# Expert weights on GpSimd's queue, and routing pieces that begin earlier in a group and lie further apart

## The chip, the core and the metric

The kernel runs on one core of one Trainium2 chip. A core has a matrix engine (TensorE, PE in the profile; its weight loads are PEld), VectorE (DVE), ScalarE (ACT), GpSimd (POOL) and SyncE (SP), which here only starts transfers. Each engine works through its own instructions in order and waits for the others by semaphores. Transfers between HBM and the on-chip memory, and within it, are started from the queue of SP, ACT or POOL and carried out by 16 DMA engines that all queues share. The metric is the device time of one execution in microseconds.

## The reference

The input x is 8 sequences of 256 tokens of width 256, in float32. Two blocks follow each other, and every sublayer adds to x:

```python
x = x + L0_xattn(layernorm(x), ctx)     # 16 heads of 16
x = x + L0_ffn(layernorm(x))            # soft mixture of 8 experts, 128 slots each
x = x + L1_xattn(layernorm(x), ctx)     # 16 heads of 64
x = x + L1_ffn(layernorm(x))            # gated square of relu
```

The change touches the second line only:

```python
xn = rmsnorm(x); sn = rmsnorm(slot_embeds)
logits   = einsum('bnd,esd->bnes', xn, sn)
dispatch = softmax(logits, over tokens n)
combine  = softmax(logits, over all e*s = 1024 slots)
slots = einsum('bnd,bnes->besd', xn, dispatch)
h     = gelu(einsum('besd,edh->besh', slots, w1) + b1)   # 256 -> 1024
eo    = einsum('besh,ehd->besd', h, w2) + b2             # 1024 -> 256
out   = einsum('bmd,bnm->bnd', eo, combine)
```

An expert has w1 and w2 of 1 MB each and b2 of 1 KB.

## The kernel before

The four sublayers run one after the other; x stays on the chip (`x_sb`). The instructions are written in a program order, and a planner then sets the order on each engine's queue: among what it holds for ready at a time, by its own estimate, the earlier in the program goes first. Only what is marked `keep_in_program_order` keeps its place. So an instruction that depends on nothing can stand much earlier in its queue than in the program, and a queue's order can differ from the code's.

**Groups.** The mixture handles the 8 sequences in 4 groups of two. All 8 experts run in each group, so each expert's weights are loaded four times. `experts(g)` gives 64 pieces, numbered n = 0 to 63, eight for an expert e. A piece is `up(e, hc)`, two products for 128 of the 1024 hidden units (L986) with a gelu on ScalarE into `ht` (L994), and one of the eight steps `down(e-1, k)` of the expert before (L1002), which waits in the list `late`. After the last step VectorE adds b2 and writes the result over `slots` (L1011).

**Weights.** There are two sets of weight buffers (`moe_sets`), used by even and odd experts, each with w1, w2 and b2. `load_second(e)` (w2 and b2: L221, L222) is written in piece 8e, `load_first(e + 1)` (w1: L218) in piece 8e + 1. All three are started from SP's queue. A load waits until TensorE has finished with the expert two before it, since that one used the same buffers. The first expert's weights are asked for at step 50 of the first sublayer's schedule, by `at(50, ...)`; they go to buffers that nothing used before.

**Routing.** `routing(g + 1)` prepares the next group's sequences (b = 0, 1 of the group) beside the experts of group g. Its steps are:

- P: normalised tokens, turned on TensorE (pt_xm).
- T: logits with tokens in rows (L851, `ln`), their maximum, an exponential on ScalarE (L862) with the reciprocal of its sum in `rzn`, and 32 x 32 transposes on VectorE (L810). The second T of a sequence also starts a *spread*: 16 transfers of 64 KB from `tk_l` to `ls` on SP's queue (L818), which bring the 32 x 32 blocks to their places.
- A: the same for the exponentials, with a spread of 16 transfers from `tk_n` to the matrix `CT` that combines the experts' outputs.
- S: softmax over tokens on half of the slots: maximum on VectorE (L893), four exponentials on ScalarE (L898), and a multiplication on GpSimd (L906).
- C: transposes back (L916) and a spread from `tk_s` to `dt`.
- F: the experts' inputs, `slots`, on TensorE (L931, `pf`) and VectorE (L941).

A sequence has two T and one A, two S and one C, and two F. A "-" in the list of steps is an empty place. `ending` holds the combining of the group before: four times eight products (L1028, `pc`) and the statistics of the next layernorm.

**Where side pieces go.** `side` is the list of ending and routing steps. One is taken after each odd n above 8; what is left over follows the last piece. With five steps of ending ahead of them in groups 1 to 3, the routing steps of groups 1 and 2 begin at n = 19; in group 0 they begin at n = 9.

Buffers that matter: `ls` and `dt` have one each; `tk`, the exponentials `em` and `rzn` two; `ph`, `pf` and `pt_xm` share three banks of the matrix engine's output memory with `pc`.

Of the kernel before, what the change touches and what calls it, by code (L numbers as in the profile page):

```python
# [14 lines left out]
P = 128  # L15
# [47 lines left out]
def kernel(ctx: ExitStack, tc: tile.TileContext, a: dict, out: bass.AP):  # L63
    nc = tc.nc
# [74 lines left out]
    def moe_mean(g):  # L139

        mv = stat.tile([P, 4, 2], F32, tag="mvp", bufs=4, name=f"mvp_moe_{g}")
        for i in range(4):
            st = stat.tile([P, 6], F32, tag="bst", bufs=4, name=f"bst_moe_{g}_{i}")
            nc.vector.bn_stats(st, x_sb[:, 4 * g + i, :])
            nc.vector.bn_aggr(mv[:, i, :], st)
        moe_stats[g] = mv

    def moe_scale(groups):


        got = []
        for g in groups:
            mv = moe_stats[g]
            roots = stat.tile([P, 2, 4], F32, tag="roots", bufs=3, name=f"roots_{g}")
            for i, (bias, scale) in enumerate(((epsb, 1.0), (0.0, float(D)))):
                tc.keep_in_program_order(
                    nc.scalar.activation(
                        roots[:, i, :], mv[:, :, 1], AF.Sqrt, bias=bias, scale=scale
                    )
                )  # L160
            got.append((g, mv, roots))
        for g, mv, roots in got:
            scl = stat.tile([P, 4], F32, tag="scl", bufs=3, name=f"scl_{g}")
            rstd = stat.tile([P, 4], F32, tag="rstdm", bufs=3, name=f"rstdm_{g}")
            nc.vector.reciprocal(rstd, roots[:, 0, :])
            nc.vector.tensor_tensor(scl, roots[:, 1, :], rstd, ALU.mult)
            nc.vector.tensor_scalar(scl, scl, 1e-12, None, ALU.max)
            nc.vector.reciprocal(scl, scl)
            nc.vector.scalar_tensor_tensor(scl, scl, 16.0, rstd, ALU.mult, ALU.mult)
            moe_stats[g] = mv, scl  # L170
# [44 lines left out]
        )  # L215

    def load_first(to, e):
        nc.sync.dma_start(to["w1"], a["w1"][e].rearrange("(c p) f -> p c f", p=P))  # L218

    def load_second(to, e):  # L220
        nc.sync.dma_start(to["w2"], a["w2"][e].rearrange("(c p) f -> p c f", p=P))  # L221
        nc.sync.dma_start(to["b2"], a["b2"][e].partition_broadcast(P))  # L222

    moe_sets = [moe_tiles(pr, 0)]
    with ExitStack() as l0:
# [534 lines left out]
        for b, plan in enumerate(  # L760
# [7 lines left out]
            does = dict(zip("PTUSDF", routing0(b)))  # L768
            for step in plan.split():
                when, _, args = step[1:].partition(".")  # L770
                at(int(when), lambda f=does[step[0]], args=args: f(*map(int, args)))
        at(50, lambda: load_first(set0, 0))
        at(50, lambda: load_second(set0, 0))

        turn_back, halves = None, []
# [23 lines left out]
    with ExitStack() as l0f:  # L799
# [22 lines left out]
        def routing(g):  # L822


            CT = moe_sets[g % 2]["CT"]
            rzn = stat.tile([P, 4], F32, tag="rzn", bufs=2, name=f"rzn_{g}")
# [3 lines left out]
            does = []  # L830
            for bl in range(2):
# [118 lines left out]
                    dict(P=prepare, T=by_token, A=turn_token, S=by_slot, C=turn_slot, F=fill)  # L950
                )

            pieces = []
            for step in (
                "P0 T00 T01 A0 P1 - S00 S01 C0 T10 T11 - F00 F01 A1 - S10 S11 C1 - - F10 F11"
            ).split():
                if step == "-":
                    pieces.append(lambda: None)
                else:
                    f, args = does[int(step[1])][step[0]], tuple(map(int, step[2:]))  # L960
                    pieces.append(lambda f=f, args=args: f(*args))
            return pieces, CT, rzn

        late = []

        def experts(g):
# [5 lines left out]
            def up(e, hc):  # L972
                w, n = moe_sets[e % 2], g * E + e

                if hc == 0 and n > 0:
                    load_second(w, e)
                if hc == 1 and n < 4 * E - 1:
                    load_first(moe_sets[(e + 1) % 2], (e + 1) % E)
                if hc == 0:
                    cur[e] = dict(w1=w["w1"], w2=w["w2"], b2=w["b2"], ht=[])  # L980
                c_ = cur[e]
                if hc % 2 == 0:
                    c_["ph"] = ps_mm(f"ph_{g}_{e}_{hc}").rearrange("p (i n) -> p i n", i=2)
                ph = c_["ph"][:, hc % 2, :]
                for c in range(2):
                    nc.tensor.matmul(  # L986
                        ph,
                        lhsT=c_["w1"][:, c, hc * P : (hc + 1) * P],
                        rhs=slots[e][:, c * 256 : (c + 1) * 256],
                        start=(c == 0),  # L990
                        stop=(c == 1),
                    )
                ht = pm.tile([P, 256], F32, tag="ht", bufs=14, name=f"ht_{g}_{e}_{hc}")
                nc.scalar.activation(ht, ph, AF.Gelu, bias=b1[:, e, hc : hc + 1])  # L994
                c_["ht"].append(ht)
# [49 lines left out]
        def finish(g, eos, CT, rzn):  # L1045
            pieces = [
                lambda bl=bl, t=t: combine(g, bl, t, eos, CT, rzn)
                for bl in range(2)
                for t in range(2)
            ]  # L1050

            def stats():
                xat_stats[g] = ln_pair(g, f"xat_{g}")

            return pieces + [stats]

        CT, rzn = set0["CT"], rzn0
        ending = []
        for g in range(4):
            work_, eos = experts(g)  # L1060
            here = (eos, CT, rzn)
            side = list(ending)
            if g < 3:
                if g == 2:
                    moe_mean(3)
                    moe_scale([3])
                pieces, CT, rzn = routing(g + 1)
                side += pieces
            for n, piece in enumerate(work_):
                piece()  # L1070
                if n % 2 == 1 and n > 8 and side:
                    side.pop(0)()
            for piece in side:
                piece()
            ending = finish(g, *here)
# [8 lines left out]
    with ExitStack() as l1:  # L1084
# [222 lines left out]
        to, qs, vs = projs[0]  # L1307
# [184 lines left out]
```

## Time and profile before

| | us |
|---|---|
| median of 3 runs | 1375.34 (1373.31 to 1376.81) |
| the profiled execution | 1375.42 |
| its span, first to last instruction | 1373.6 |
| TensorE busy | 1302.9 (95%) |
| VectorE busy | 572.2 (42%) |
| ScalarE busy | 564.2 (41%) |
| GpSimd busy | 194.8 (14%) |
| first expert product to last combining product | 283 to 912 |

The profile is one execution. In its lists of instructions each line gives the start in us from the span's beginning, the duration, engine, line of the kernel, operation, output<-input and count; brackets hold the idle time before it and what ended that. An engine name with q is that engine's queue: instructions that only start a transfer or wait. A line of waits reads: who waited, for whom, us in total, how often, the longest. In the strips of digits each digit is the busy share of a fortieth of the span in tenths.

### The profile page before, as it was taken

What the parts mean: (1) busy time and instruction counts of PE and PEld (TensorE: products, weight loads), DVE (VectorE), ACT (ScalarE), POOL (GpSimd) and SP (SyncE); (2) the same over time, 40 slices, a digit from 0 to 9 for tenths busy, and PEclk for the clock granted to TensorE, in tenths of its full rate; (3) what the DMA queues carried; (4) which work ended last, traced back from release to release, by engine and by line L of the source; (5) the groups of instructions that cost most, each with busy time, mean ns of one, the idle gap of its engine ahead of it and who ended that gap; (6) DMA issues with size and microseconds to landing.
All of it is one profiled execution on the core that took longest, in us unless ns stands there. A gap on an engine that the chain in (4) does not pass through costs nothing.

```text
span 1373.6 us, 18749 instructions
## 1 busy us (share of the span) xinstructions
PE 1302.9 (95%) x7216; PEld 937.8 (68%) x7216; DVE 572.2 (42%) x1160; ACT 564.2 (41%) x1374; POOL 194.8 (14%) x149
## 2 busy tenths in 40 slices
PE   6999999899989999799998999999999999999988
PEld 3566665466667877578767788866667667577767
DVE  5777777533311234221350210025444544554544
ACT  1445454636322245322553122204544544544643
POOL 1000001101010001100011000013332422323514
PEclk8899999999999999999998999999999999999999
DMA  8000000025664435752467524240000000000001
GB/s 259 14 2 1 1 2 1 1 96 142 183 171 144 131 98 146 190 190 82 119 166 186 169 93 168 100 126 0 1 1 1 1 1 1 1 1 1 1 31 54
DMA packets 125161, 105.72 MB, mean 77 GB/s; under 512 B 57105, under 2 KB 115089, under 8 KB 125073
## 3 DMA queue, kind: packets, MB, share of 16 engines
q1 hardware_dynamic: 123488, 103.22, 25.4%
q10 hardware_dynamic: 1584, 1.31, 0.4%
q8 instruction: 57, 0.93, 0.3%
q14 instruction: 32, 0.25, 0.1%
HBM read 83.53 MB, written 2.10 MB: 62 GB/s over the span
## 4 chain that ended last, share of the span: by engine, by line
PE 70%; SPq 9%; DMA 7%; ACT 6%; DVE 5%; issue 2%; POOL 1%; POOLq 0%; ACTq 0%; DVEq 0%
PE ph L986 11%; PE pe L1002 11%; SPq L818 8%; PE sc L73 8%; PE q L73 6%; PE o L73 5%; PE po L73 5%; PE k L73 5%; PE pc L1028 4%; DMA w<-in_w_dram 4%; PE v L73 4%; PE pe L76 4%; PE pf L931 2%; ACT ex L1228 2%; PE ln L851 1%
## 5 line engine op out<-in xcount | busy, mean ns | idle before, releaser
L994 ACT ACTIVATE ht<-ph,b 128x256 f32<-128x256 f32 x256 | 118.3, 474 | 386.7 <-PE ph L986 385.6
L1002 PE MATMUL pe<-w,ht 128*128 128x256 f32 x1024 | 262.5, 389 | 13.9 <-DMA w<-in_w_dram 13.9
L986 PE MATMUL ph<-slots,w 128*128 128x256 f32 x1024 | 264.6, 386 | 11.3 <-ACT ht L994 5.4
L986 PEld LDWEIGHTS ph<-slots,w 128*128 128x128 f32 x1024 | 187.7, 191 | 67.5 <-ACT ht L994 26.2
L1002 PEld LDWEIGHTS pe<-w,ht 128*128 128x128 f32 x1024 | 197.2, 194 | 48.4 <-issue 10.1
L1241 POOL TENSOR_TENSOR ex<-ex,rz 128x1024 f32<-128x1024 f32 x64 | 120.2, 1899 | 224.1 <-DVE rz L1239 219.5
L1228 ACT ACTIVATE ex<-sc,nm 128x256 f32<-128x256 f32 x256 | 117.4, 484 | 45.2 <-DVE nm L1223 44.0
L1011 DVE TENSOR_TENSOR slots<-pe,b 128x512 f32<-128x512 f32 x32 | 22.1, 691 | 269.1 <-PE pe L1002 269.1
L73 PE MATMUL sc<-KT,QT 17*128 17x256 f32 (+1 forms) x1024 | 106.3, 385 | 5.5 <-DVE NM L488 3.6
L499 ACT ACTIVATE ex<-sc 128x512 f32<-128x512 f32 x128 | 74.7, 597 | 83.8 <-PE sc L73 76.0
L488 DVE TENSOR_REDUCE NM<-sc 128x2 f32<-128x512 f32 x128 | 86.7, 687 | 31.8 <-PE sc L73 27.4
L73 PEld LDWEIGHTS sc<-KT,QT 17*128 17x128 f32 (+1 forms) x1024 | 78.0, 189 | 28.3 <-issue 13.3
L73 PE MATMUL q<-xT,wq 128*128 128x256 f32 x384 | 94.8, 395 | 0.9 <-ACT V L1193 0.9
L73 PEld LDWEIGHTS q<-xT,wq 128*128 128x128 f32 x384 | 70.9, 192 | 26.4 <-issue 12.1
L906 POOL TENSOR_TENSOR ls<-ls,zs 128x1024 f32<-128x1024 f32 x12 | 22.7, 1894 | 430.2 <-DMA CT<-tk_n 364.2
L1223 DVE TENSOR_REDUCE nm<-sc 128x4 f32<-128x1024 f32 x64 | 75.4, 1219 | 6.5 <-PE sc L73 2.8
L73 PE MATMUL po<-wo,ot 128*128 128x256 f32 x320 | 72.6, 382 | 0.0
L76 PE MATMUL pe<-ident,ex 128*128 128x128 f32 x512 | 69.9, 278 | 0.5 <-DVE xT L1143 0.4
L73 PEld LDWEIGHTS po<-wo,ot 128*128 128x128 f32 x320 | 60.1, 190 | 11.3 <-issue 3.6
L1257 ACT COPY et<-pe 128x512 f32<-128x512 f32 x64 | 37.1, 608 | 72.0 <-PE pe L76 71.7
L76 PEld LDWEIGHTS pe<-ident,ex 128*128 128x128 f32 x512 | 56.2, 140 | 14.1 <-issue 8.0
L73 PE MATMUL o<-et,V 128*64 128x256 f32 x512 | 62.8, 385 | 0.9 <-ACT ot L1276 0.9
(180 smaller groups left out, 1551.3 us busy)
## 6 DMA issues: line engine op xcount, KB each, us to landing
w<-in_w_dram SPq DMA_DIRECT2D x64, 1024.0 KB, 7.1
ls<-tk_l SPq DMA_DIRECT2D x96, 64.0 KB, 2.0
CT<-tk_n SPq DMA_DIRECT2D x96, 64.0 KB, 2.1
dt<-tk_s SPq DMA_DIRECT2D x96, 64.0 KB, 2.9
b<-in_b_dram SPq DMA_DIRECT2D x32, 128.0 KB, 6.9
out_dram<-y SPq DMA_DIRECT2D x8, 256.0 KB, 2.1
x_sb<-in_x_dram SPq DMA_DIRECT2D x3, 512.0 KB, 6.9
ctx0T<-in_ctxT_dram SPq DMA_DIRECT2D x4, 256.0 KB, 6.0
```

Source lines behind the costliest of these rows:

```text
L73: tc.keep_in_program_order(nc.tensor.matmul(out, lhsT=lhsT, rhs=rhs, start=start, stop=stop))
L76: tc.keep_in_program_order(nc.tensor.transpose(out, in_, ident))
L488: nc.vector.tensor_reduce(NMs[(2 * b + t // 2) % 2][:, qb, t, HD0 + 1 + 64 * i : 64 * i + 64 : 32], sc[i][:, :, 0, :], AX.X, ALU.max, nega ...
L499: nc.scalar.activation(ex[:, 2 - 2 * i : 4 - 2 * i, :], sc[1 - i][:, :, 1, :], AF.Exp)
L818: nc.sync.dma_start(to(32 * k, a), tk[32 * a : 32 * a + 32, k, :, :, :].rearrange(rows))
L986: nc.tensor.matmul(ph, lhsT=c_["w1"][:, c, hc * P : (hc + 1) * P], rhs=slots[e][:, c * 256 : (c + 1) * 256], start=(c == 0), stop=(c == 1),)
L994: nc.scalar.activation(ht, ph, AF.Gelu, bias=b1[:, e, hc : hc + 1])
L1002: nc.tensor.matmul(c_["pe"][:, b, :], lhsT=c_["ht"][hc][:, b * SL : (b + 1) * SL], rhs=c_["w2"][:, hc, :], start=(hc == 0), stop=(hc == HI ...
L1028: nc.tensor.matmul(pc[:, :D], lhsT=CT[:, bl, e, t * P : (t + 1) * P], rhs=eos[e][:, bl, :], start=(e == 0), stop=(e == E - 1),)
L1223: nc.vector.tensor_reduce(nm, sc, AX.X, ALU.max, negate=True)
L1228: nc.scalar.activation(ex[:, i, qb, :], sc[:, i, qb, :], AF.Exp, bias=nm[:, i, qb : qb + 1], accum_out=z[:, i, qb : qb + 1],)
L1241: nc.gpsimd.tensor_tensor(ex, ex, rz.rearrange("p h q -> p (h q)").unsqueeze(2).to_broadcast([P, 4, S]), ALU.mult,)
```

## The change

`load_first` and `load_second` start their three transfers from GpSimd's queue instead of SP's, for all experts and groups.

The list of routing steps is split. P0, T00 and T01 (the first sequence's tokens and logits) form `first`, which goes ahead of the ending of the group before; the rest follows the ending. In groups 0 to 2 side pieces are taken after each odd n above 2 instead of above 8, so that `first` stands after n = 3, 5 and 7 and three more places exist. They are used for further empty places in the list: one after S01, one between T10 and T11, one between S10 and S11 and one more after C1, while the one between T11 and F00 goes. In group 3, which has no routing, pieces are still taken from n = 9.

```diff
     def load_first(to, e):
-        nc.sync.dma_start(to["w1"], a["w1"][e].rearrange("(c p) f -> p c f", p=P))
+        nc.gpsimd.dma_start(to["w1"], a["w1"][e].rearrange("(c p) f -> p c f", p=P))
 
     def load_second(to, e):
-        nc.sync.dma_start(to["w2"], a["w2"][e].rearrange("(c p) f -> p c f", p=P))
-        nc.sync.dma_start(to["b2"], a["b2"][e].partition_broadcast(P))
+        nc.gpsimd.dma_start(to["w2"], a["w2"][e].rearrange("(c p) f -> p c f", p=P))
+        nc.gpsimd.dma_start(to["b2"], a["b2"][e].partition_broadcast(P))
...
+            def piece(step):
+                if step == "-":
+                    return lambda: None
+                f, args = does[int(step[1])][step[0]], tuple(map(int, step[2:]))
+                return lambda: f(*args)
+
+            first = [piece(step) for step in ("P0", "T00", "T01")]
             pieces = []
             for step in (
-                "P0 T00 T01 A0 P1 - S00 S01 C0 T10 T11 - F00 F01 A1 - S10 S11 C1 - - F10 F11"
+                "A0 P1 - S00 S01 - C0 T10 - T11 F00 F01 A1 - S10 - S11 C1 - - - F10 F11"
             ).split():
-                if step == "-":
-                    pieces.append(lambda: None)
-                else:
-                    f, args = does[int(step[1])][step[0]], tuple(map(int, step[2:]))
-                    pieces.append(lambda f=f, args=args: f(*args))
-            return pieces, CT, rzn
+                pieces.append(piece(step))
+            return first, pieces, CT, rzn
...
-                pieces, CT, rzn = routing(g + 1)
-                side += pieces
+                first, pieces, CT, rzn = routing(g + 1)
+                side = first + side + pieces
             for n, piece in enumerate(work_):
                 piece()
-                if n % 2 == 1 and n > 8 and side:
+                if n % 2 == 1 and (n > 8 or (n > 2 and g < 3)) and side:
                     side.pop(0)()
```

## The prediction

> **What bounds the kernel now.** The page first: which engine is busy, and in which slices it isn't.
>
> ```profile
> PE 1302.9 (95%) x7216; PEld 937.8 (68%) x7216; DVE 572.2 (42%) x1160; ACT 564.2 (41%) x1374; POOL 194.8 (14%) x149
> ...
> PE   6999999899989999799998999999999999999988
> ...
> DMA  8000000025664435752467524240000000000001
> ```
>
> TensorE is the bound: 1302.9 of 1373.6 us. A change pays only where TensorE stands still or runs slowly. The holes lie in slice 1, where the DMA engines are full, and around slices 10 to 22, the expert stage. The waits of TensorE in that stage (276 to 912 us) come next:
>
> ```profile
> PE pe L1002 <- DMA w<-in_w_dram: 13.9, 6, 2.8
> PE ph L986 <- ACT ht L994: 5.4, 5, 3.0
> PE ph L986 <- DMA w<-in_w_dram: 4.9, 3, 3.4
> ```
>
> So 18.8 us in nine waits are for expert weights, 5.4 for ScalarE. Why weights come late is seen in SP's instructions in order of time (start, duration, line, transfer, count):
>
> ```profile
> 541.42 10.17 SPq L818 DMA_DIRECT2D ls<-tk_l  x16
> 551.70 0.53 SPq L221 DMA_DIRECT2D w<-in_w_dram  x1
> ...
> 552.91 0.43 SPq L218 DMA_DIRECT2D w<-in_w_dram  x1
> 553.45 16.09 SPq L818 DMA_DIRECT2D CT<-tk_n  x16
> 569.63 0.56 SPq L221 DMA_DIRECT2D w<-in_w_dram  x1
> ```
>
> One routing spread is 16 small transfers at about 0.63 us of SP each, 10.2 us. The weight transfers of 569.63 stood behind such a spread (and this one took 16.09 us: in the waits of SP's queue L818 waits 17.6 us in nine waits for landing weights). TensorE, in order of time, in the same stretch:
>
> ```profile
> 557.59 4.15 PE L1002 MATMUL pe<-w,ht 128*128 128x256 f32 x18 [2.35 <-DMA w<-in_w_dram]
> 562.72 2.83 PE L986 MATMUL ph<-slots,w 128*128 128x256 f32 x12 [0.98 <-DMA w<-in_w_dram]
> ...
> 567.55 1.89 PE L986 MATMUL ph<-slots,w 128*128 128x256 f32 x8
> ...
> 576.08 3.53 PE L1002 MATMUL pe<-w,ht 128*128 128x256 f32 x8 [2.79 <-DMA w<-in_w_dram]
> ```
>
> Weights asked for at 569.63 land at 575.94, and TensorE starts at 576.08. It also pays twice: eight matmuls take 1.89 us at 567.55 and 3.53 us after the wait, with a granted clock of 0.57 between 576 and 580 us. In the stage 34 matmuls of 256 columns start 0.425 us apart, where 2106 start 0.215 apart: 34 x 0.21 = 7.1 us more.
>
> **The change part by part.** The durations are of the profiled execution: 1375.42 us, of which 1373.6 are the span. The median of the runs is 1375.34, so the sum can be read against either.
>
> (1) *Weights leave SP's queue.* 64 transfers of 1 MB and 32 of b2 move from SP to GpSimd's queue; none is added. SP keeps the 288 spread transfers and nothing stands behind them any more that TensorE waits for soon. What can go is 18.8 us of waits and the 7.1 us of slow clock, 25.9. The weights still share the DMA engines with the spreads. A spread alone moves 1 MB in 10.2 us, about 100 GB/s; loads have moved near 300 GB/s at full share. An expert (2.23 MB) then has about 200 GB/s while a spread runs, 11 us, against 14.1 us for eight pieces (820.74 to 834.83). It fits, barely where spreads follow each other: I leave 4 us of the waits standing. Gain 22.
>
> Here a rule of the Trainium skill speaks against the change. DMA: Bandwidth & Descriptors, section "Issuing engines are not separate DMA queues", says that starting DMAs on several engines saves only the sequencer's issue time, usually small beside the transfer. By that rule alone part 1 is worth about 0. The row above says that the sequencer's time is not small here: 10.2 us of issue stand ahead of a load that lands 6.3 us after it starts. I take the row.
>
> (2) *What GpSimd's queue then holds.* Six pairs of 1.9 us multiplies (L906) in the stage, 22.7 us, and now three transfers for an expert. The trace shows no DMA of GpSimd. From below: SP's row, 0.37 + 0.37 + 0.34 = 1.1 us for an expert. From above: the same page ("Specifications") gives about 1 us to the first byte for GpSimd's kind, 0.6 for SP's; three of them are an estimate of 3 us. I take 3. In a clear stretch there is room: w1 starts at 820.07, w2 lands at 829.3, both are needed from 834.83 on, so 5.5 us are spare. Cost 0 as long as that spare lasts; beyond it, each microsecond is paid by every expert in a clear stretch. In order, a load waits on this queue for TensorE to free the buffer (SP's L218 spent 259.2 us so), and an L906 behind it waits too. Loads are freed within a piece or two of where L906 stands in the order, so its follower, the C spread, is late by 1 to 3 us; it has 8 pieces until F. The other way round, an L906 in front whose ScalarE chain takes some 7 us (330.42 to 337.97 for two) can hold a load by 1 to 2 us beyond the spare; that is in the 4 us above.
>
> The page SBUF — State Buffer, "Summary: rules for kernel authors", advises SP's kind over GpSimd's beside VectorE, which in its fast mode shuts GpSimd out while descriptors are written. VectorE is busy 153.66 of 636.30 us here and one instruction lasts 0.4 to 1.2 us, so a load is put off by about one instruction: 1.2 us of the spare of 5.5. By the rule taken at its worst for every load it is still 0 in the sum.
>
> (3) *Routing pieces earlier and further apart.* The pieces are the same, so TensorE's own work is unchanged. Spreads go to pieces 7, 19, 31, 37, 43, 53 of groups 1 and 2 where they stood at 23, 25, 35, 39, 47, 55 (group 0: 7, 9, 21, 27, 33, 43 instead of 13, 15, 25, 29, 37, 45). From C0 to F00 it stays 8 pieces plus two T pieces, from C1 to F10 it becomes 8 pieces (13.9 us and more) instead of 6, against 2.4 us of transposes, 10.2 of issue and 1.4 to land. ScalarE: the wait of 2.99 us at 338.5 (group 0) stands behind eight exponentials and six table loads between 330.4 and 344.4; apart, that clump shrinks. If S10 and S11 no longer share a table, three times two loads of 1.28 us are added, hidden under ScalarE's 66% idle time in the stage; uncovered they would cost 7.7. I take 3 us gain of the 5.4, bounds -3 to +5. A wait is added: rzn has two buffers, so in groups 1 and 2 T's reciprocal (0.16 us) must come after the combines at pieces 9 to 15, which read the same buffer two groups on. Only later combines read it, and the combines' own VectorE work has to stand ahead of it in the queue, so it holds up nothing: 0. In group 2, P0 at piece 3 (some 5 us in) needs the statistics whose Sqrt table is loaded 1.8 us before the group starts: 0, at most 2 us once.
>
> (4) *The first expert's weights.* This one is easily missed. They depend on nothing, and were held back to 27.00 us only because SP's queue was full of start-up loads. The chain of waits there is DMA:
>
> ```profile
> 12.37 7.12 DMA ctx0T<-in_ctxT_dram
> 19.51 4.73 DMA ctx1T<-in_ctxT_dram
> 24.71 5.53 DMA se<-in_slots_dram
> ```
>
> GpSimd's queue is free from 4.1 us on (its last memset of the start), so 2.23 MB are likely to start there, and the DMA share is 0.76 to 1.06 from 2 to 24 us: the bytes push all loads behind them, by 2.23 MB / 300 GB/s = 7.4 us. The slot embeddings (se, landed 30.24) gate VectorE and then TensorE at 35.22; they had about 2 us of w1 beside them, which goes. Cost 5.5 us, bounds 0 (the order written for the queue puts them late) and 8.
>
> **Sum.** -22 - 3 + 5.5 = -19.5 us: 1375.4 - 19.5 = 1356.
>
> **The rivals.** *A, the transfers are the limit.* For: w1 started at 388.75 beside a dt spread took 10.1 us without standing behind anything, and the DMA share is 0.7 to 0.96 in such stretches. Against: only 18 spreads of 10.2 us in the 482 us of three groups, mean share 0.52 to 0.54. If half of the waits stay, part 1 gives 10, part 3 nothing: 1375.4 - 10 + 5.5 = 1371.
>
> *B, GpSimd writes the descriptors too slowly (ends slower).* w2 is 1024 rows of 1 KB. If an expert's three transfers hold GpSimd for more than the spare 5.5 us, the next weights are late by the rest, in about 15 experts without side work on TensorE (group 3 has no wait for weights today and would get them). Zero net at 5.5 + 19.5/15 = 6.8 us; at 8 us, 15 x 2.5 = 37.5 lost, 1393. For: no run shows this cost. Against: it must be six times SP's 1.1 us.
>
> *C, the order doesn't move.* The program's order is only a priority; SP already ran w1 ahead of w2 although the code has it behind, so the pieces could stay near where they were. Then part 3 is 0 and the rest holds: 1359, within the likeliest case.
>
> **How the numbers follow.** Likeliest case with C: 0.78, own range 1342 to 1369. A: 0.09, straddling the bound. B: 0.13. About 0.3% (4 us) is what this measurement can tell from no change. Faster 0.80, same 0.07, slower 0.13. The range runs from 1342 (start-up free, all waits gone) to 1377, which leaves out B and little else.
>
> **What would show it.** Right: TensorE's waits for w in the stage under 5 us and hardly a slow matmul; every spread on SP near 10.2 us, none of 14 to 16; DMA rows on GpSimd of about 1 us; first expert matmul to last combine 605 us instead of 629; the first expert's loads near 4 us and se landing at 35 or 36. Wrong: DMA rows on GpSimd of 3 us and more with waits for w in group 3 (B), or loads that take 10 us and more beside spreads with the waits in place (A).

## The result, and the profile after

The changed kernel takes 1393.3 us in the median of four runs (1388.8 to 1394.7), the kernel before 1374.3 on the same chip: a ratio of 1.013 with an interval of 1.0101 to 1.0159. It is slower by some 18 us, where 19 faster was forecast. The profiled execution took 1394.68 us with a span of 1392.9 us.

From the page of the changed kernel, in the order of the lines shown of before: busy time, the strips of TensorE and of the DMA engines, and then the rows of the two DMA queues (packets, MB, share of the 16 engines).

```profile
PE 1307.6 (94%) x7216; PEld 936.8 (67%) x7216; DVE 572.5 (41%) x1160; ACT 639.3 (46%) x1432; POOL 264.3 (19%) x245
...
PE   5899999899898999889998999999999999999988
...
DMA  8000000027652465643565424340000000000011
...
q0 software_dynamic: 18944, 71.31, 15.7%
q1 hardware_dynamic: 76896, 31.91, 10.0%
```

TensorE does the same 7216 products. ScalarE has 58 instructions and 75 us more, though the change adds it no work. The weights (71 MB) now lie on a queue of their own; the spreads and most other loads stay on q1.

The stage boundaries are the first expert product and the last combining product. They split the loss of 19.3 us of the profiled executions: start-up 283.1 to 291.3 us (+8.2), expert stage 629.2 to 637.8 (+8.6), the rest 461.3 to 463.8 (+2.5). TensorE's waits in the expert stage of the changed kernel:

```profile
PE ph L991 <- ACT ht L999: 15.2, 11, 3.1
PE pf L931 <- DMA dt<-tk_s: 9.8, 2, 5.0
PE pe L1007 <- DVE slots L1016: 5.5, 7, 0.8
PE pe L1007 <- ACT ht L999: 1.5, 1, 1.5
```

The 18.8 us for weights are gone to the last one. In their place stand 16.7 us for ScalarE (5.4 before), 9.8 us for a routing spread (none before) and 5.5 us in seven small waits for VectorE (none before): 32.0 against 24.2, which is nearly all of the stage's 8.6 us.

**Start-up.** GpSimd's queue, SP's queue, ScalarE with its queue, and TensorE of the changed kernel, in order of time:

```profile
4.09 0.87 POOL L218 DMA_DIRECT2D w<-in_w_dram  x1
4.95 0.92 POOL L221 DMA_DIRECT2D w<-in_w_dram  x1
5.86 0.56 POOL L222 DMA_DIRECT2D b<-in_b_dram  x1
```

```profile
3.95 0.37 SPq L107 DMA_DIRECT2D x_sb<-in_x_dram  x1
...
32.24 0.42 SPq L286 DMA_DIRECT2D se<-in_slots_dram  x1
```

```profile
12.24 0.35 ACTq L244 DMA_DIRECT2D wk<-in_wk_dram  x1
...
16.22 0.35 ACTq L249 DMA_DIRECT2D maskb<-in_mask_dram  x1
16.62 0.30 ACT L132 ACTIVATE rstdp_l<-mvp_l,epsb 128x2 f32<-128x2 f32 x1 [13.89 <-DMA wq<-in_wq_dram]
```

```profile
17.70 1.14 PE L76 MATMUL pt_x<-ident,xh_l 128*128 128x128 f32 x4 [8.53 <-DVE xh_l L177]
```

and the same square root and products before the change:

```profile
9.81 0.29 ACT L132 ACTIVATE rstdp_l<-mvp_l,epsb 128x2 f32<-128x2 f32 x1 [7.11 <-DMA wq<-in_wq_dram]
```

```profile
10.89 0.78 PE L76 MATMUL pt_x<-ident,xh_l 128*128 128x128 f32 x4 [1.68 <-DVE xh_l L177]
```

The first expert's weights go out at 4.09 us, beside the loads that the first sublayer needs at once. TensorE then stands 8.53 us instead of 1.68. It is not the first sequence's data that is late: it landed at 4.13 us (4.21 before), and VectorE had finished its statistics by 5.4 in both kernels. Late is ScalarE's square root of them (L132), at 16.62 instead of 9.81. In ScalarE's order it stands behind four more starts of loads, and in the trace such a start comes just after an earlier transfer has landed: L244 at 12.24, after the x transfer of 3.95, which landed at 12.22 (7.52 before), and L249 at 16.22, after one that landed at 16.20. With the weights beside them these transfers take longer, that x transfer 8.3 us instead of 3.8. SP's queue stands in the same way and slips by 7.5 us: the slot embeddings start at 32.24 instead of 24.71.

**ScalarE.** A stretch of group 1 in the changed kernel, in order of time; L898 is an exponential of S, L999 a gelu:

```profile
504.66 1.28 ACT L898 ACT_TABLE_LOAD   x1
505.95 0.51 ACT L898 ACTIVATE ls<-ls,nms 128x256 f32<-128x256 f32 x1
506.37 0.19 ACT L898 ACTIVATION_READ_ACCUMULATOR ls<-ls,nms 128x1 f32 x1
506.57 1.28 ACT L999 ACT_TABLE_LOAD   x1
507.87 0.84 ACT L999 ACTIVATE ht<-ph,b 128x256 f32<-128x256 f32 x2
508.72 1.28 ACT L898 ACT_TABLE_LOAD   x1
```

One exponential and two gelus come to 4.06 us here (508.72 - 504.66), 2.57 of them for two table loads. TensorE needs two gelus every 3.52 us (a quarter of the 14.09 us for eight pieces). So ScalarE, idle for more than half of the span, falls behind while the two kinds alternate. In this stretch that still costs nothing: TensorE has no wait between 486 and 530 us. It waits at the group's end, where exponentials of S and gelus still alternate:

```profile
584.96 1.13 PE L991 MATMUL ph<-slots,w 128*128 128x256 f32 x4 [1.21 <-ACT ht L999]
...
589.15 1.13 PE L991 MATMUL ph<-slots,w 128*128 128x256 f32 x4 [2.63 <-ACT ht L999]
```

Between the gelu that ends at 584.90 and the next, which ends at 589.09, ScalarE does two table loads and two exponentials. The table loads of the stage, before and then after (count, busy us, mean ns):

```profile
L994 ACT ACT_TABLE_LOAD x23 | 29.5, 1283 | 7.8 <-PE ph L986 7.5
...
L898 ACT ACT_TABLE_LOAD x6 | 7.7, 1283 | 0.1
```

```profile
L999 ACT ACT_TABLE_LOAD x52 | 66.7, 1283 | 9.9 <-PE ph L991 9.0
L898 ACT ACT_TABLE_LOAD x35 | 44.9, 1283 | 12.9 <-DVE nms L893 7.6 <-DMA CT<-tk_n 4.8
```

29 became 87. That exponentials and gelus use different tables is also what the Trainium skill says (ScalarE: Activation LUTs, "Table sets: the hidden batching unit": each set has one expensive function, and changing between sets costs a load); the count is what this order makes of it.

**The spread at a group's end.** SP, GpSimd, TensorE, and two windows with the granted clock, DMA share and GB/s in the last three columns, all of the changed kernel:

```profile
591.97 12.38 SPq L818 DMA_DIRECT2D dt<-tk_s  x16
```

```profile
592.77 0.74 POOL L218 DMA_DIRECT2D w<-in_w_dram  x1 [3.27 <-PE ph L991]
601.40 0.92 POOL L221 DMA_DIRECT2D w<-in_w_dram  x1 [7.89 <-PE pe L1007]
```

```profile
609.51 6.64 PE L931 MATMUL pf<-dt,xh_moe 128*128 128x512 f32 x8 [4.78 <-DMA dt<-tk_s]
```

```profile
609.00:613.00 4.00, 3.48 (x4) 0.50 0.00 0
...
605.00:609.00 4.00, 0.00 (x0) 0.96 0.81 257
```

SP had issued the last of the sixteen small transfers at 604.35 (591.97 + 12.38), and it landed 5.0 us later (1.4 to 1.6 us in every dt spread of before; here and below, a spread's landing is counted from the end of its issue). Between 605 and 609 us the DMA engines are 81% busy with weights that nobody needs yet, and TensorE does nothing. Then the clock is at 0.50 and eight products take 6.64 us that take 3.60 elsewhere. So one wait costs 4.78 + 3.04 us.

### The profile page after: what moved, and what is told of

It reads as the page before. It is cut to its first block, busy times and chain, and to the rows that moved or that the text cites. A ratio compares the mean times of both kernels' runs of the same rounds, so it can differ in the third digit from the quotient of the medians.

```text
span 1392.9 us, 18836 instructions
## 1 busy us (share of the span) xinstructions
PE 1307.6 (94%) x7216; PEld 936.8 (67%) x7216; DVE 572.5 (41%) x1160; ACT 639.3 (46%) x1432; POOL 264.3 (19%) x245
## 3 DMA queue, kind: packets, MB, share of 16 engines
q0 software_dynamic: 18944, 71.31, 15.7%
q1 hardware_dynamic: 76896, 31.91, 10.0%
## 4 chain that ended last, share of the span: by engine, by line
PE 71%; ACT 10%; DMA 8%; DVE 5%; issue 3%; SPq 2%; POOL 1%; POOLq 0%; ACTq 0%; DVEq 0%
PE ph L991 12%; PE pe L1007 10%; PE sc L73 8%; PE q L73 6%; PE o L73 5%; PE po L73 5%; PE k L73 5%; PE v L73 4%; PE pe L76 4%; PE pc L1033 3%; PE ln L851 3%; PE pf L931 2%; SPq L818 2%; DMA dt<-tk_s 2%; ACT ex L1233 2%
## 5 line engine op out<-in xcount | busy, mean ns | idle before, releaser
L999 ACT ACTIVATE ht<-ph,b 128x256 f32<-128x256 f32 x256 | 116.2, 472 | 306.2 <-PE ph L991 305.5
L1007 PEld LDWEIGHTS pe<-w,ht 128*128 128x128 f32 x1024 | 193.7, 191 | 41.4 <-DVE slots L1016 13.4
L1016 DVE TENSOR_TENSOR slots<-pe,b 128x512 f32<-128x512 f32 x32 | 22.0, 687 | 180.8 <-PE pe L1007 180.8
L73 PEld LDWEIGHTS q<-xT,wq 128*128 128x128 f32 x384 | 71.1, 193 | 27.2 <-issue 13.6
L218 POOL DMA_DIRECT2D w<-in_w_dram x32 | 22.8, 714 | 274.9 <-PE ph L991 255.4
```

The costliest lines, as they stand in the source:

```text
L73: tc.keep_in_program_order(nc.tensor.matmul(out, lhsT=lhsT, rhs=rhs, start=start, stop=stop))
L1007: nc.tensor.matmul(c_["pe"][:, b, :], lhsT=c_["ht"][hc][:, b * SL : (b + 1) * SL], rhs=c_["w2"][:, hc, :], start=(hc == 0), stop=(hc == HI ...
```

## The experiments

Three theories came out of this profile. *Start-up*: early weights delay the first loads. *Tables*: the order of exponentials and gelus got worse. *Ring*: loads on a queue of their own no longer stand behind a spread but beside it, and slow it. The rival of all three is the one on record: GpSimd itself is too slow. Its DMA rows speak against it from the start: 0.7, 0.9 and 0.56 us, 2.2 us for an expert.

**One part alone.** First, the kernel before with the three loads on GpSimd's queue and nothing else changed.

```diff
-        nc.sync.dma_start(to["w1"], ...
+        nc.gpsimd.dma_start(to["w1"], ...
```

> Loads on GpSimd's queue, routing as in the kernel before. Theory (two new costs: the first expert's weights in the start-up traffic, and ScalarE's tables): start-up about 8 us later, no wait of TensorE for weights (18.8 us and some 7 us of slow clock less), function tables 53 instead of 29 in the stage for L898 and gelu (18 + 35), so some 8 of the 20 us that the 87 of the changed kernel cost: about 1366 us. Rival (GpSimd's queue itself is the loss, by holding loads behind multiplications and the reverse): at or above 1390 us, since all loads are on that queue here too.

Measured: 1409.1 us, ratio 1.0217 (1.0192 to 1.0243). A miss in sign. The waits of TensorE in its stage:

```profile
PE ph L986 <- ACT ht L994: 19.5, 10, 3.6
PE pf L931 <- DMA dt<-tk_s: 10.5, 3, 5.2
PE pe L1002 <- DVE slots L1011: 5.5, 7, 0.8
```

The queue alone brings all three new waits, and takes those for weights away. A fourth row, 5.2 us for L931 with no releaser named, is the same wait for dt in group 0: F10 starts at 417.84, and the spread had landed at 417.65. With 33 us the loads alone lose more than the whole change. The time would fit the rival, which named 1390 or more; against it stand GpSimd's short rows and the missing waits for weights, and later e9, which has all loads but the first expert's on GpSimd and is faster than the kernel before.

Then the new routing list alone, with the loads left on SP (`load_first` and `load_second` as before).

> Routing earlier and further apart, loads on SP's queue as before. Theory: no start-up cost; 82 tables for L898 and gelu (33 + 49), nearly those of the changed kernel, so ScalarE and the late dt spread cost about 20 us; the waits for weights stay in part (10 to 19 us): 1375 + 10 to 20 = 1385 to 1395. Rival (GpSimd's queue is the loss): 1375 or less, as nothing is on that queue and the spreads are spaced.

Measured: 1376.5 us, 0.9993 (0.9979 to 1.0006). Also a miss, the other way: the list by itself costs nothing and gains nothing.

```profile
PE ph L991 <- ACT ht L999: 21.6, 10, 6.3
...
PE ph L991 <- DMA w<-in_w_dram: 0.9, 1, 0.9
```

The new list alone removes 17.9 of the 18.8 us for weights, on SP's old queue. ScalarE takes nearly all of it back (21.6 us, 5.4 before), with 82 table loads for L898 and L999 together. The move of the loads had almost no wait for weights left to remove.

**The start-up loads.** The changed kernel, with the first expert's weights on SP as before.

```diff
-        at(50, lambda: load_first(set0, 0))
-        at(50, lambda: load_second(set0, 0))
+        at(50, lambda: load_first(set0, 0, nc.sync))
+        at(50, lambda: load_second(set0, 0, nc.sync))
```

> The changed kernel, with only the two loads of step 50 (first expert, 2.1 MB) back on SP's queue. Theory: the whole start-up loss returns, slot embeddings land near 30.2 us again instead of 37.7, and the rest is as in the changed kernel: 1393 - 8 = 1385. Rival (start-up delay is absorbed later): 1393.

Measured: 1387.4 us, 1.0069 (1.0046 to 1.0093). The first expert product comes at 284.6 us instead of 291.3. As expected in the median, though the twelve runs lie between 1378 and 1394. The profiled one took 1392.5: in its stage F10 waits for dt in all three groups, 15.6 us, instead of in two.

**The order of gelus and exponentials.** The changed kernel, with both kinds of ScalarE instruction held in the order in which the program states them.

```diff
-                        nc.scalar.activation(      # L898, exponentials of S
+                        tc.keep_in_program_order(nc.scalar.activation(
...
-                nc.scalar.activation(ht, ph, AF.Gelu, ...)
+                tc.keep_in_program_order(nc.scalar.activation(ht, ph, AF.Gelu, ...))
```

> The changed kernel, with gelu and the exponentials of S kept in program order on ScalarE: 41 tables for L898 and gelu instead of 87, all else alike. Theory: TensorE's waits for ScalarE fall from 15.2 to about 5 us, those for the dt spread from 9.8 to about 0, with their slow clock of some 6 us: 1393 - 20 = 1373. Rival (the late dt comes from GpSimd's queue, where L906 stands behind loads, or from spreads slowed by loads): waits for dt stay near 10 us and the time within 5 us of 1393.

Measured: 1380.9 us, 1.0029 (1.0018 to 1.0040). That is 12 to 14 us less than the changed kernel (by medians and by ratios), with 41 table loads for the two lines instead of 87. The size is less than was expected, because the other wait grew:

```profile
PE pf L931 <- DMA dt<-tk_s: 15.8, 3, 5.6
PE ph L991 <- ACT ht L999: 5.2, 8, 1.9
```

F10 stands in front of the late spread in all three groups instead of two. The kept order need not be the reason: e3, with its 87 table loads, has the same three waits.

The same edit on the kernel before:

> The kernel before with gelu and the exponentials of S in program order (39 tables instead of 29), nothing else. Theory: weights still stand behind spreads, so the 25 us of waits stay: 1372 to 1382. Rival (order on ScalarE alone is worth much, whatever the routing): under 1368.

Measured: 1402.5 us, 1.0188 (1.0169 to 1.0206), a miss. TensorE waits 39.0 us for gelus, in fifteen waits. A fixed order is no gain by itself: in the old list the exponentials stand close behind the spread that they need, and a gelu that stands behind them in the fixed order waits too. ScalarE's own waits agree in part: before L898's tables it stands 10.4 us for spreads, in three waits, with gelus behind it.

**The queue, with the order kept.** Now both spoilers are taken out. First with the loads on SP, then with the loads of all but the first expert on GpSimd, both with the new routing list and the order kept; they differ in the queue alone.

> Loads on SP's queue as before, routing as in the changed kernel, gelu and the exponentials of S kept in program order (41 tables instead of 82). Theory (routing alone takes the waits for weights away, and the tables ate the gain): waits for ScalarE fall from 21.9 us to about 5, nothing takes their place: 1376 - 16 = about 1360. Rival (the waits only change their name): waits for weights or for dt come back, 1370 to 1376.

Measured: **1358.7 us**, 0.9876 (0.9859 to 0.9892), as expected. It beats both kernels of the case. The reason holds only in part: TensorE still waits 13.6 us for gelus, where about 5 were expected (21.6 in e2). Most of the rest of the gain is speed: TensorE is busy for 596.0 us of the stage instead of 602.6, at a granted clock of 0.99 instead of 0.98.

```profile
PE ph L991 <- ACT ht L999: 13.6, 13, 3.5
```

> The changed kernel with both remedies: first expert's loads on SP, and order kept. Theory (the two costs add): 1381 - 6 = 1375; TensorE's waits for dt stay near 15 us, so that e5, which differs only in the loads' queue, is faster by some 15 us. Rival (queue of the loads is neutral once the two costs are away): e6 within 4 us of e5.

Measured: 1374.6 us, 0.9994 (0.9984 to 1.0004), as expected. Beside e5 on the same chip the queue costs 15.8 us.

```profile
PE pf L931 <- DMA dt<-tk_s: 16.9, 3, 6.5
PE ph L991 <- ACT ht L999: 4.6, 7, 1.9
```

SP in e5, and TensorE there, at the end of group 1:

```profile
568.56 10.72 SPq L818 DMA_DIRECT2D dt<-tk_s  x16
579.38 0.53 SPq L221 DMA_DIRECT2D w<-in_w_dram  x1
```

```profile
581.02 3.60 PE L931 MATMUL pf<-dt,xh_moe 128*128 128x512 f32 x8
```

and the same products in e6, whose spread was started at 573.91 us, with weights begun at 574.69 and 584.21 on the other queue:

```profile
592.11 6.05 PE L931 MATMUL pf<-dt,xh_moe 128*128 128x512 f32 x8 [4.56 <-DMA dt<-tk_s]
```

From the start of the spread to F10 it takes 12.5 us in e5, without a wait, and 18.2 us in e6. SP's queue is what protects the spread: the weights stand behind it and can't start before 579.38. This is the very order that the change was to undo. Three waits of 4.6 to 6.5 us make 16.9 us. They are not the loss by themselves: the waits for gelus are 9.0 us shorter in e6, but eight products take 1.7 to 2.5 us more after each wait, and the first expert product comes 2.6 us later (286.6 against 284.0).

Last, the same stage with hardly any loads: e4, but only the first group loads its experts' weights (on GpSimd's queue). The later groups leave their loads out and compute with what lies in the buffers, so the output is not that of the reference.

> As e4 (loads on GpSimd, order kept), but experts' weights are loaded in group 0 only; the later groups compute with what lies in the two sets, so 48 of 64 large transfers are left out. Theory (the loads on a ring of their own slow the spreads): a spread of dt takes 10.2 us of SP and lands 1.5 us after in groups 1 and 2, TensorE's waits for dt there fall from 10.2 us to under 3, and the time from 1381 to about 1370. Rival (dt is late only because TensorE comes earlier to F): the waits in groups 1 and 2 stay near 5 us each and the time within 3 us of 1381.

Measured: 1365.0 us, 0.9927 (0.9905 to 0.9950), 14 to 16 us less than e4.

```profile
PE pf L931 <- DMA dt<-tk_s: 6.1, 1, 6.1
```

The one wait left is that of group 0, where loads run. In groups 1 and 2 the last dt transfer lands 1.4 us after its issue, where it took 5 to 6 at the ends of these groups in e4. So the loads, not SP or the spread's own size, make it late. The Trainium skill has a mechanism that fits (DMA: Bandwidth & Descriptors, "Queues, rings and completion order"): each DMA engine takes turns between the queues that have work for it, packet by packet. A packet of weights, as the profile counts them, is 3.8 KB here (71.31 MB in 18944), one of q1 0.4 KB (31.91 MB in 76896). No run here looks inside an engine; what is shown is that the delay comes and goes with the loads beside the spread.

**More distance.** If F10 merely comes too soon for a slower spread, C1 can be moved forward. The next two are e6 and e5 with piece A1 behind C1, which puts C1 four pieces earlier.

```diff
-  ... T11 F00 F01 A1 - S10 - S11 C1 - - - F10 F11
+  ... T11 F00 F01 - S10 S11 C1 A1 - - - - F10 F11
```

> As e6 (loads of the later experts on GpSimd's queue, first expert on SP's, program order kept between the gelus and the exponentials of S), with the schedule's piece A1 moved from before S10 to behind C1, so that C1 stands two pairs of entries earlier and more pieces lie between C1 and F10. Theory (the waits of 16.9 us for dt are a spread that lands late because loads share the transfer engines with it, and F10 is too near to it): the waits for dt fall under 6 us, and the time is about 1364 to 1369. Rival (the loads on their own queue cost something else than this wait, and the 16.9 us only show it): the waits move to another instruction and the time stays at 1372 to 1377.

Measured: 1363.7 us, 0.9910 (0.9884 to 0.9937): 10.9 us better than e6. The wait fell less than expected, to 8.8 us; the profile writes it on CT, but F reads dt, and F10 starts 0.35 us after dt's spread has landed, in all three groups.

```profile
PE pf L931 <- DMA CT<-tk_n: 8.8, 3, 3.2
PE ph L991 <- ACT ht L999: 8.5, 12, 2.3
```

> As e5 (all loads on SP's queue, program order kept), with the same move of A1 behind C1. e5 has no wait for dt, so by the theory the move gains nothing here: 1356 to 1361. If it gained as much as in e9, the move would be worth something for another reason than the late dt, and e9 would say nothing on the queue. A loss is possible if S10 and S11 side by side make ScalarE late at one more place: up to 1366.

Measured: 1371.9 us, 0.9972 (0.9959 to 0.9985): 13.1 us *worse* than e5, a miss. SP and TensorE of this kernel:

```profile
569.08 10.74 SPq L818 DMA_DIRECT2D dt<-tk_s  x16
579.92 10.67 SPq L818 DMA_DIRECT2D CT<-tk_n  x16
590.69 0.56 SPq L221 DMA_DIRECT2D w<-in_w_dram  x1
```

```profile
596.51 3.36 PE L1007 MATMUL pe<-w,ht 128*128 128x256 f32 x8 [3.42 <-DVE xh_l L177]
...
601.29 1.97 PE L991 MATMUL ph<-slots,w 128*128 128x256 f32 x8 [1.42 <-DMA w<-in_w_dram]
```

C1 and A1 follow each other, so the weights stand behind two spreads, 21.6 us. The w2 load of 590.69 landed at 596.37, and TensorE starts at 596.51: this is a wait for weights, although the row names VectorE. It is the fault that the prediction found in the kernel before. The two moves make a square (us; the kernel before took 1375.4 beside the left column and 1376.5 beside the right):

| | A1 before S10 | A1 behind C1 |
|---|---|---|
| loads on SP | 1358.7 | 1371.9 |
| later experts' loads on GpSimd | 1374.6 | 1363.7 |

Beside a list with single spreads the change of queue costs 16 us; beside one with two spreads in a row it gains 8.

One more pair of pieces between C1 and F10, on e9:

```diff
-  A0 P1 - S00 S01 - C0 T10 - T11 F00 F01 - S10 S11 C1 A1 - - - - F10 F11
+  A0 P1 - S00 S01 C0 - T10 T11 F00 F01 - S10 S11 C1 A1 - - - - - F10 F11
```

> As e9, with one more pair of pieces (about 4 us) between C1 and F10: C0, T11, F00, F01, S10, S11, C1 and A1 each one entry earlier, so every other distance stays. Theory (F10 comes too soon for a spread that lands late beside loads): the 8.8 us that F10 still waits in e9 (2.8 in each of three groups) fall under 2, with the slow clock behind each wait, and the time goes from 1363.7 to 1353 to 1358. Rival (the wait follows F10, because the spread itself starts later or lasts longer as soon as more loads fall beside it): the wait stays over 6 us and the time at 1361 to 1366.

Measured: 1361.8 us, 0.9900 (0.9879 to 0.9922). The wait of F10 is gone, but the theory is only half right. At the ends of groups 1 and 2 the spread now lands 7.0 and 7.2 us after its issue (4.3 and 4.2 in e9), so 2 to 3 us of the added distance are used up, much as the rival said, and F10 starts 0.35 us after the landing. The time missed its range by 4 us: waits for gelus went from 8.5 to 13.3 us. e5 stays the best.

## Why the prediction was wrong

By ratios to before, e5 is the change without its faults: 0.9876. From there to the changed kernel are 2.54%, 35 us: 16 for the queue in the stage (e6 against e5), 5 to 8 for the start-up (e4 against e6, and the changed kernel against e3), and 10 to 14 for the tables (e3 against e6, and the changed kernel against e4). Each of the last two has two values as it was taken out first or second.

**(1) and (2), gain 22 at no cost: the step that failed first.** The waits for weights did go, all 18.8 us. The 7.1 us of slow clock did not: TensorE is busy for 605.6 us of the stage, 603.9 before, since it now slows behind other waits. And (1) asked only what a spread does to a load, "An expert (2.23 MB) then has about 200 GB/s while a spread runs", and never what a load does to a spread. F10 was costed with "1.4 to land", a number taken from rows in which the queue kept the next weights behind the spread. Beside loads it is 5 us and more at the ends of the groups, a cost that the sum does not have. Nor was there cover for it: 2.4 + 10.2 + 1.4 us already fill the "13.9 us and more" of the eight pieces, and 10.2 is the shortest issue, where the dt spreads of before took 12.2 to 16.7. With list and order alike the queue lost 15.8 us (e6 against e5) where it was to gain 22. The rule that the prediction weighed and set aside (another queue saves only the time of issue, usually small) was nearer in size than the row that it preferred, and still not right: the change of queue is worth anything between -8 and +16 us here. The row itself, 10.2 us of issue ahead of a load, was read rightly, but it did not follow that only another queue could help: the new list alone leaves 0.9 us of waits for weights (e2).

The estimate in (2), 3 us of GpSimd for an expert, was fair: 2.2. Nor did VectorE visibly hold its loads up: the rows of w1 stay between 0.70 and 0.87 us throughout. Rival B named 1393 us, which is what came out, but that is luck: no wait for weights is left, in group 3 or elsewhere. Rival A, that the transfers are the limit, was nearer in kind: loads and spreads did stand in each other's way, but it was the spread that paid and not the load.

**(3), gain 3 with at most six more table loads: failed in size and sign, 10 to 14 us lost.** 58 more loads came, 74 us of ScalarE, and the waits for it went from 5.4 to 16.7 us. The list alone brings 53 of them (e2: 82 loads), the queue alone 24 (e1: 53). The step counted the pieces in the order of the list, although rival C says itself that the list is only a priority. It also took 66% idle time as cover. Cover has to be had where the loads fall: 4.06 us of ScalarE do not fit into 3.52 of expert pieces, and still less where one gelu only stands between two switches (4.19 us from 584.90 to 589.09). Why the planner alternates is argued, not shown: after the change an exponential is ready while gelus are still coming, so that they are taken in turn.

**(4), cost 5.5: right, a little low.** The profile has 8.2 us, the medians 5 to 8. The bytes and the early start were right: all later loads slip, the slot embeddings by 7.5 us where 7.4 was reckoned. Two things were not. The 2 us that se was to win back did not come: it took 5.45 us to land instead of 5.53, so it landed at 37.69 and not at 35 or 36. And TensorE was held first on a path that the step does not have, by ScalarE's square root behind its late load starts (8.53 us).

**Of the signs named**, no waits for w, DMA rows of about 1 us and loads near 4 us came true. Spreads near 10.2 us did not (mean 13.3 us of issue, 12.8 before), nor the stage of 605 us (637.8).

**Open**: the seven waits of 0.78 us for VectorE at L1016, which were not tried by themselves, and 2.5 us after the stage, where the waits are the same as before.

## What to carry to other kernels

Before a stream of large loads is taken off the queue on which small urgent transfers stand, ask what the queue's order was good for in both directions: it may hold loads back behind a spread, and thereby keep the spread fast. Look first whether more distance in the schedule, on the old queue, removes the same wait. An engine's idle share covers added work only within the period of the engine that it feeds, so count table switches in the order that was really built, and hold back a load that depends on nothing: here it ran in the start-up and cost 5 to 8 us.

## What the hardware showed

In the changed kernel a transfer of 1 MB costs GpSimd 0.70 to 0.95 us of its own time, and one of 128 KB 0.56 to 0.60 us; before, they cost SP 0.37 and 0.55 us in the median. Weights from either queue land about as fast (median 6.8 us from GpSimd, 7.1 from SP). A spread's last 64 KB land 1.4 us after their issue when no loads run beside it (e7) and up to 9 us after it beside loads of another queue (A0's spread in group 1 of e11: 9.1). After a wait of 4.78 us the profile shows TensorE at a granted clock of 0.50 for 4 us and 0.58 for the next 3; its eight products took 6.64 us instead of 3.60.
